# A graph-attention layer on one core: which operands of five vector steps lie in PSUM, and who issues the row loads and how the products are cut at the end

## The chip, the core and the metric

The kernel runs on one core of a Trainium2 chip. A core has five engines that run their own instruction streams: TensorE (PE, matrix products from SBUF into PSUM), VectorE (DVE), ScalarE (ACT), GpSimd (POOL) and SyncE (SP, which here only issues DMAs). SBUF and PSUM are the two on-chip memories of 128 partitions each. ACT and SP can also issue plain DMAs, one instruction each; POOL issues the indirect ones, which gather 128 rows of a table by 128 indices. Engines wait for each other through semaphores. The metric is device time in microseconds (us) of one launch; the median over several runs counts.

## The reference

One attention layer over a graph of 12,500 nodes and 412,500 edges that are sorted by their target, added to its input:

```python
h = jnp.maximum(_layernorm(x), 0.0)
h = (h @ W_node.T).reshape(N, 4, 32)
e = (edge_attr @ W_edge.T).reshape(E, 4, 32)
att = jnp.sum(jnp.concatenate([h[src], h[tgt], e], -1) * a, -1)
att = jnp.where(att > 0, att, 0.2 * att)
m = jnp.maximum(segment_max(att, tgt), 0.0)
ex = jnp.exp(att - m[tgt])
denom = segment_sum(ex, tgt) + (E - deg)[:, None] * jnp.exp(-m)
out = x + segment_sum((ex / denom[tgt])[:, :, None] * h[src], tgt)
```

The `0.2` is the leaky step that the change touches. The maximum per target is subtracted before the exponential, so sums of different pieces of one target have to be rescaled when they meet.

## The kernel before

**Data.** A preparation stage writes a table of one row per node (144 floats, 576 bytes): four heads of 32 projected features, two ones and a logit part (35 numbers per head, `AW`), and four more numbers per node. The edges are cut into 461 chunks of 7 tiles of 128 edges. Seven chunks are a batch (49 tiles); there are 66 batches, numbers 0 to 65, and the last has six chunks, the last of which has three tiles.

**Loading rows.** For each tile the 128 source rows come into a tile `hs`, of which there are three in a ring, so batch b+1 is loaded while b is worked on and the slot of b+1 was that of b-2. Most tiles are gathered by POOL (line 636 in `gather`, one indirect DMA each); ahead of a batch's gathers POOL does a tiny memset `gate` (line 631), which waits for the products of batch b-2. From batch 3 on the first tile of each odd batch and the first two of each even batch (the last batch: one) are instead loaded row by row with plain DMAs of 576 bytes (line 662 in `row_by_row`; line 658 loads 32 addresses into registers). Of each batch's 128 or 256 such rows, ACT issues 80 (`ACTROWS`) at the end of the iteration two before, SP the others: up to 64 at the start of the iteration before, then what is left, and with what remains of 112 those of the batch after next.

**One iteration b of the main loop**, in the order in which the code is written, which is also the order on each engine: SP's first rows of batch b+1, then its loads of `lw` for b+1 (line 585), POOL's gathers of b+1, SP's edge features for b+2, SP's other rows; then `weigh(b)`, which waits on DVE for the rows (line 670) and makes the weights; `load_pen` (SP, line 677), which has one buffer `pen_sb` and so waits for `weigh(b)`; `mark` (one-hot matrices, line 714); `scatter(b)` (DVE scales the rows, line 822, PE sums them per target, line 829); `spread` and `choose` for b+1 (lines 594 to 611); `begin(b+2)` (PE, edge logits into PSUM `z`, line 695). The sums of b-1 are copied by ACT within `weigh(b)` (`collect`, line 851) and merged into `acc` by `merge` every second batch; in the last four iterations that have it (from b = 62) `collect` and `close` of batch b itself stand at the end of iteration b, ahead of ACT's row issues for b+2. `finish` turns completed nodes into output.

**weigh_part** works on 32 partitions by 896 edges: four additions `att = z + zst` (line 751), the leaky step into `z` (754), a forward and a backward segmented maximum `up` and `m` (757, 759), a subtraction (760), four exponentials on ACT (762), four break products `both[.., 1]` from `pen` and `m` (766), transposes (768, 770). `z` and `up` are in PSUM, the others in SBUF.

**merge** makes decay factors `f` in the PSUM tile named "up", `scale` in SBUF, multiplies the sums `r` by `scale` (879), scans (881), writes products `put` in SBUF (888, 891) and adds them to two columns of `acc` per chunk (900).

**The last batch** (65) is weighed and multiplied in two parts, tiles 0 to 3 and 4 to 6, in `end_in_parts`: DVE scales the rows (796), PE makes one product of 32 by 140 per chunk and tile (802), and ACT copies it head by head, 32 by 35 each (810).

Of the kernel before, what the change touches and what calls it, by code (L numbers as in the profile page):

```python
# [14 lines left out]
OP = mybir.AluOpType  # L15
# [75 lines left out]
def by_row(b):  # L91

    return (2 if b % EVERY == 0 and b < NBT - 1 else 1) if LOOSE < b < NBT else 0


def merges():
# [36 lines left out]
def kernel(  # L133
# [603 lines left out]
    def weigh_part(s, t0, t1, before):  # L737

        zst, att, up, m, both = s.zst, s.att, s.up, s.m, s.both
        own = s.hs[:, :, :EROW].rearrange("p (t q) (h k) -> p t q h k", t=T, h=H)[:, t0:t1, :s.chunks, :, AW - 1]  # L740
        e0, e1 = t0 * P, t1 * P

        def grouped(what, g):
            return what.rearrange("r (t g i) -> r g t i", g=NQT, i=R)[:, g, t0:t1, :]

        nc.vector.tensor_tensor(logits[:, t0:t1, :s.chunks * H].rearrange("p t (q h) -> p t q h", h=H),  # L746
                                own, pick[:, t0:t1, :s.chunks, :H], op=OP.add)
        nc.vector.transpose(zst[:, t0:t1, :].rearrange("p t i -> p (t i)"),  # L748
                            logits[:, t0:t1, :].rearrange("p t i -> p (t i)"))
        for g in range(NQT):  # L750
            on_half(s, nc.vector.tensor_tensor(grouped(att, g), grouped(s.z, g),  # L751
                                               zst[g * R:(g + 1) * R, t0:t1, :], op=OP.add))
        z = s.z[:, e0:e1]
        on_half(s, nc.vector.scalar_tensor_tensor(z, att[:, e0:e1], 0.2, att[:, e0:e1], op0=OP.mult, op1=OP.max))  # L754
# [5 lines left out]
        on_half(s, nc.vector.tensor_tensor(att[:, e0:e1], z, mp, op=OP.subtract))  # L760
        for g in range(NQT):
            nc.scalar.activation(both[g * R:(g + 1) * R, 0, t0:t1, :], grouped(att, g), AF.Exp)  # L762
        if before:
            collect(before, 1)
        for g in range(NQT):
            nc.vector.scalar_tensor_tensor(both[g * R:(g + 1) * R, 1, t0:t1, :], grouped(s.pen[:, 1:], g), -1.0 / BIG,  # L766
                                           grouped(m, g), op0=OP.mult, op1=OP.mult)
        nc.vector.transpose(ex_ps[:, t0:t1, :].rearrange("p t r -> p (t r)"),  # L768
                            both[:, 0, t0:t1, :].rearrange("p t r -> p (t r)"))
        nc.vector.transpose(zst[:, t0:t1, :].rearrange("p t r -> p (t r)"),  # L770
                            both[:, 1, t0:t1, :].rearrange("p t r -> p (t r)"))
        nc.vector.tensor_copy(own, zst[:, t0:t1, :s.chunks * H].rearrange("p t (q h) -> p t q h", h=H))

    def end_in_parts(s):

        nc.vector.memset(s.pen[:, EARLY * P:EARLY * P + 1], -BIG)
        spans = ((0, EARLY), (EARLY, T))
        r = work.tile([P, AW * (MC + 1)], F32, name="r")
        r = r[:, :AW * (len(spans) * s.chunks + 1)].rearrange("p (d c) -> p d c", d=AW)
        breaks = work.tile([P, s.chunks, len(spans)], F32, name="breaks")  # L780
        nc.vector.memset(breaks, 0.0)
        nc.vector.tensor_copy(breaks[:, :, 0], new[:, s.c0:s.c0 + s.chunks])
        by_chunk = s.hs[:, :, :EROW].rearrange("p (t q) k -> p q t k", q=CB)
        for i, (t0, t1) in enumerate(spans):
            if i:
                landed(nc.vector, "late", late_sems, late_done, 0, s.hs[:, EARLY * CB:, :], s.ends[:, :, :, :])
                weigh_part(s, t0, t1, None)
            else:
                weigh(s, None)
            got = []  # L790
            for q in range(s.chunks):
                held = min(tiles_of(s.c0 + q), t1)
                if held <= t0:
                    continue
                rows = by_chunk[:, q, t0:held, :].rearrange("p t (h k) -> p t h k", h=H)[:, :, :, :HB]
                nc.vector.tensor_tensor(
                    rows, rows, ex_ps[:, t0:held, q * H:(q + 1) * H, None].to_broadcast([P, held - t0, H, HB]), op=OP.mult)
                if q % G == 0:
                    pa = ps.tile([P, RUN], F32, name="pa", bufs=3)
                at = q % G * W  # L800
                for t in range(t0, held):
                    nc.tensor.matmul(pa[at:at + W, :EROW], s.hot[:, t, q, :], s.hs[:, t * CB + q, :EROW],
                                     start=(t == t0), stop=(t == held - 1), tile_position=(0, at))
                got.append((q, pa[at:at + W, :]))
            for q in range(s.chunks):
                if tiles_of(s.c0 + q) <= t0:
                    nc.vector.memset(r[:, :, 1 + q * len(spans) + i], 0.0)
            for q, pa in got:
                for h in range(H):
                    nc.scalar.copy(r[h * W:(h + 1) * W, :, 1 + q * len(spans) + i], pa[:, h * AW:(h + 1) * AW])  # L810
        return r, breaks

    def scatter(s):
# [39 lines left out]
    def merge(c0, count, r, breaks=None):  # L853
# [2 lines left out]
        step = n // count  # L856
        breaks = new[:, c0:c0 + n] if breaks is None else breaks.rearrange("p c k -> p (c k)")
        flat = (AW - 1) * (n + 1)
        f = ps.tile([P, BANKS * 512], F32, name="up")[:, :flat].rearrange("p (d c) -> p d c", d=AW - 1)
        nc.vector.memset(f[:, :, 0], 0.0)  # L860
        m = r[:, AW - 1, 1:n + 1]
        run = work.tile([P, MC + 1], F32, name="run")
# [8 lines left out]
        nc.vector.tensor_tensor(dif[:, 0, :n], dif[:, 0, :n], breaks, op=OP.add)  # L871
        nc.vector.tensor_tensor(dif[:, 1, :n], m, run[:, 1:n + 1], op=OP.subtract)
        nc.scalar.activation(f[:, :HD + 1, 1:n + 1], dif[:, 0, None, :n].to_broadcast([P, HD + 1, n]), AF.Exp)
        scale = work.tile([P, MC], F32, name="scale")
        nc.scalar.activation(scale[:, :n], dif[:, 1, :n], AF.Exp)
        nc.vector.tensor_scalar(f[:, HD + 1, 1:n + 1], breaks, 1.0 / BIG, 1.0, op0=OP.mult, op1=OP.add)
        nc.vector.tensor_copy(r[:, :AW - 1, 0], carry)
# [196 lines left out]
    with tc.manual_schedule():  # L1074
# [15 lines left out]
        for b in range(NBT - 1):  # L1090
# [332 lines left out]
```

## Time and profile before

| what | value |
|---|---|
| median of 3 runs | 4031.48 us (4031.11 to 4036.24) |
| the profiled execution's own time | 4038.12 us |
| its span, first to last instruction | 4036.3 us |
| mean granted clock of TensorE | 0.679 |
| busy: POOL / DVE / PE / ACT | 75% / 59% / 36% / 22% of the span |

The profile is of one execution. A row of a group of instructions gives source line, engine, operation, output and inputs, count, then busy us and mean ns of one, then the idle time of the engine just before them and what ended it. A row of the timeline gives start and duration in us, engine, line, operation, output and inputs, count, and in brackets the idle time before it. SPq and ACTq are DMA issues on those engines' queues. The span's start is time zero in all of them.

### The profile page before, as it was taken

The numbers are of one execution on the slowest core, as the hardware profiler recorded it, in microseconds if no ns is written. First come the engines' busy times: TensorE is split into PE (matmuls) and PEld (weight loads), VectorE is DVE, ScalarE is ACT, GpSimd is POOL, SyncE is SP. The second block draws the span as 40 slices with busy tenths as digits, with TensorE's granted clock in tenths as the row PEclk, the third lists the DMA queues.
The fourth block names the chain that finished last, engine by engine and source line by source line (L and its number), as shares of the span: only waits on it lengthen the run. The fifth ranks groups of instructions, "written<-read, shape, count | busy, mean of one in ns | idle before, by whom it ended". The sixth has DMA issues, their size and how long they took to land.

```text
span 4036.3 us, 45376 instructions
## 1 busy us (share of the span) xinstructions
PE 1471.9 (36%) x3512; PEld 577.0 (14%) x3512; DVE 2379.0 (59%) x4319; ACT 875.2 (22%) x2714; POOL 3011.5 (75%) x3205
## 2 busy tenths in 40 slices
PE   5653334443243243333233234234323324324322
PEld 4311111111011011111011111111101101101101
DVE  8676666656555556546546646555655555655565
ACT  5232221222122212212212212212212211211222
POOL 7777777777777777777777777777777777777771
PEclk8776667776676676677576667666667667667666
DMA  8444444434434443334443343443443444343430
GB/s 223 121 102 114 117 109 110 101 93 103 109 90 109 108 110 91 101 88 107 108 110 93 100 103 91 108 109 95 99 107 90 105 108 109 87 105 89 109 92 23
DMA packets 287741, 418.29 MB, mean 104 GB/s; under 512 B 83154, under 2 KB 204430, under 8 KB 287410
## 3 DMA queue, kind: packets, MB, share of 16 engines
q0 software_dynamic: 100128, 230.32, 25.1%
q1 hardware_dynamic: 163696, 174.62, 14.8%
q10 hardware_dynamic: 23586, 10.39, 1.1%
q14 instruction: 301, 2.47, 0.2%
q8 instruction: 30, 0.49, 0.1%
HBM read 399.53 MB, written 15.51 MB: 103 GB/s over the span
## 4 chain that ended last, share of the span: by engine, by line
POOL 50%; issue 19%; DVE 6%; SPq 6%; ACTq 5%; PE 4%; ACT 2%; DMA 1%; DVEq 0%; POOLq 0%
POOL hs L636 50%; ACTq L662 4%; SPq L662 4%; PE pa L829 3%; DVE hs L822 2%; PE z L695 1%; SPq L658 1%; ACTq L658 1%; DMA hs<-table,ends 1%; ACT r L851 1%; ACT both L762 1%; DVE pick L611 1%; DVE hot L714 1%; DVE acc L900 1%; ACT up L986 1%
## 5 line engine op out<-in xcount | busy, mean ns | idle before, releaser
L636 POOL DMA_INDIRECT hs<-table,ends x3062 | 2938.8, 960 | 928.3 <-issue 924.7
L829 PE MATMUL pa<-hs,hot 128*128 128x502 f32 x1820 | 926.2, 673 | 2411.8 <-DVE hs L822 2333.8
L829 PEld LDWEIGHTS pa<-hs,hot 128*128 128x128 f32 x1820 | 396.3, 222 | 2933.8 <-issue 2863.7
L851 ACT COPY r<-pa 32x35 f32<-32x35 f32 x1820 | 380.0, 209 | 1968.7 <-issue 1882.8
L746 DVE TENSOR_TENSOR logits<-hs,pick 128x196 f32<-128x196 f32 (+1 forms) x67 | 32.9, 491 | 1017.2 <-DVEq L670 1016.6
L822 DVE TENSOR_TENSOR hs<-hs,exr 128x924 f32<-128x924 f32 x455 | 472.3, 1107 | 0.0
L695 PE MATMUL z<-eft,wa 128*32 128x512 f32 (+3 forms) x1056 | 443.6, 556 | 28.3 <-DMA eft<-in_ef 28.3
L611 DVE COPY_PREDICATED pick<-exr,lw 128x3136 f32<-128x3136 int32 x66 | 239.8, 3633 | 47.4 <-ACT pick L594 47.3
L611 DVE COPY_PREDICATED pick<-exr,pick 128x1568 f32<-128x1568 int32 (+3 forms) x198 | 230.6, 1165 | 6.8
L762 ACT ACTIVATE both<-a 32x224 f32<-32x224 f32 (+2 forms) x268 | 103.2, 385 | 599.2 <-DVE a L760 529.1
L594 ACT COPY pick<-lw 128x3136 f32<-128x3136 f32 x66 | 184.8, 2800 | 81.8 <-ACTq L670 80.3
L768 DVE STREAM_TRANSPOSE exr<-both 128x224 f32<-128x224 f32 (+1 forms) x67 | 28.3, 423 | 236.0 <-ACT both L762 236.0
L695 PEld LDWEIGHTS z<-eft,wa 128*32 128x32 f32 (+1 forms) x1056 | 95.6, 110 | 378.6 <-issue 353.7
L900 DVE TENSOR_TENSOR acc<-acc,a 128x70 f32 x461 | 108.0, 234 | 69.2 <-issue 50.9
L757 DVE TENSOR_TENSOR_SCAN up<-pen_sb,z 32x896 f32<-32x896 f32 (+1 forms) x67 | 133.3, 1990 | 11.9 <-DMA pen_sb<-pens 9.6
L714 DVE TENSOR_TENSOR hot<-exr,key 128x448 f32<-128x448 f32 (+1 forms) x260 | 129.0, 558 | 9.3 <-PE pa L829 2.3
L759 DVE TENSOR_TENSOR_SCAN m<-pen_sb,up 32x896 f32<-32x896 f32 (+1 forms) x67 | 132.6, 1979 | 2.3
L751 DVE TENSOR_TENSOR a<-z,zst 32x224 f32<-32x224 f32 (+2 forms) x268 | 101.0, 377 | 9.9 <-DVE zst L748 0.5
L766 DVE SCALAR_TENSOR_TENSOR both<-pen_sb,m 32x224 f32<-32x224 f32 (+2 forms) x268 | 100.8, 376 | 2.7
L986 ACT COPY up<-a 32x224 f32<-32x224 f32 (+1 forms) x224 | 74.5, 332 | 35.4 <-DVE a L978 28.7
L246 POOL DMA_INDIRECT hs<-in_x,ends x67 | 63.5, 948 | 20.5 <-issue 20.1
L754 DVE SCALAR_TENSOR_TENSOR z<-a 32x896 f32<-32x896 f32 (+1 forms) x67 | 72.1, 1075 | 2.3
(187 smaller groups left out, 1057.0 us busy)
## 6 DMA issues: line engine op xcount, KB each, us to landing
hs<-table SPq DMA_DIRECT2D x6992, 0.6 KB
eft<-in_ef SPq DMA_DIRECT2D x66, 1344.0 KB
hs<-table ACTq DMA_DIRECT2D x5040, 0.6 KB
hs<-table,ends POOLq DMA_INDIRECT x3062, 2.6
lw<-near SPq DMA_DIRECT2D x461, 64.0 KB
eft<-in_ef SPq DMA_DIRECT2D x66, 224.0 KB
pen_sb<-pens SPq DMA_DIRECT2D x66, 98.1 KB
table<-rows ACTq DMA_DIRECT2D x9, 648.0 KB
```

Of the source, the lines that this page charges most:

```text
L594: nc.scalar.copy(pick[:, :, :s.chunks, :], lw[:, None, :s.chunks, :n].to_broadcast([P, T, s.chunks, n]))
L611: nc.vector.copy_predicated(pick[:, :, :s.chunks, :n], bit[:, :, :, None].to_broadcast([P, T, s.chunks, n]), more)
L636: load = nc.gpsimd.indirect_dma_start(out=s.hs[:n, t * CB + q, :], out_offset=None, in_=table[:, :], in_offset=bass.IndirectOffsetOnAxis(a ...
L662: by_itself(engine.dma_start(s.hs[i % P:i % P + 1, i // P, :].bitcast(U8), table_b[ds(v, WIDE)].rearrange("(o c) -> o c", o=1)), f"lone{s. ...
L695: s.made = own_half(s, nc.tensor.matmul(s.z[:, part], wa3[:n, j, :], s.eft[:n, j, part], start=(j == 0), stop=(j == SB - 1)))
L714: nc.vector.tensor_tensor(s.hot[:, :, q0:q0 + n, :].rearrange("p t q r -> p q t r"), rows_ps[:, None, None, :].to_broadcast([P, n, T, W]), ...
L757: on_half(s, nc.vector.tensor_tensor_scan(up[:, e0:e1], s.pen[:, e0:e1], z, 0.0, op0=OP.add, op1=OP.max))
L762: nc.scalar.activation(both[g * R:(g + 1) * R, 0, t0:t1, :], grouped(att, g), AF.Exp)
L822: nc.vector.tensor_tensor(rows, rows, ex_ps[:, :, q * H:(q + 1) * H, None].to_broadcast([P, T, H, HB]), op=OP.mult)
L829: scattered[s.b] = nc.tensor.matmul(pa, s.hot[:, t, q0:q0 + G, :].rearrange("p q r -> p (q r)"), flat[:, at:at + RUN], start=(t == 0), sto ...
L851: nc.scalar.copy(to, pa[row:row + W, k:k + AW])
L900: nc.vector.tensor_tensor(cols, cols, put[:, i0 + i, :, :], op=OP.add)
```

## The change

Four vector steps get one of their two SBUF inputs into PSUM, the leaky step is cut in two for it, and two things change in the last batches:

- `weigh_part`: the sum of logits goes to the PSUM tile `up`; the leaky step becomes a multiplication `att = 0.2 * up` and a maximum of `up` and `att`; the break products read `up` (the forward maximum) where they read `m`, which is the same number wherever `pen` isn't zero.
- `merge`: `scale` and `put` lie in the PSUM tile "up".
- rows: `act_rows` gives ACT 40 rows of batch 64 and none of batch 65, instead of 80 of each; SP issues the others. SP's counts become 64 + 40 + 8 in iteration 63 (64 + 48 before) and 64 + 56 in iteration 64 (none before); its 112 in iteration 62 stay.
- `end_in_parts`: each product of 32 by 140 becomes four of 32 by 35, one per head, written to the head's own 32 partitions, with all chunks of a part side by side in one PSUM tile; ACT copies a part with one instruction, that of the first part after the second part's exponentials.

```diff
+def act_rows(b):
+    return ACTROWS if b < NBT - 2 else ACTROWS // 2 if b < NBT - 1 else 0
...
         for g in range(NQT):
-            on_half(s, nc.vector.tensor_tensor(grouped(att, g), grouped(s.z, g),
+            on_half(s, nc.vector.tensor_tensor(grouped(up, g), grouped(s.z, g),
                                                zst[g * R:(g + 1) * R, t0:t1, :], op=OP.add))
         z = s.z[:, e0:e1]
-        on_half(s, nc.vector.scalar_tensor_tensor(z, att[:, e0:e1], 0.2, att[:, e0:e1], op0=OP.mult, op1=OP.max))
+        nc.vector.tensor_scalar(att[:, e0:e1], up[:, e0:e1], 0.2, None, op0=OP.mult)
+        on_half(s, nc.vector.tensor_tensor(z, up[:, e0:e1], att[:, e0:e1], op=OP.max))
...
             nc.vector.scalar_tensor_tensor(both[g * R:(g + 1) * R, 1, t0:t1, :], grouped(s.pen[:, 1:], g), -1.0 / BIG,
-                                           grouped(m, g), op0=OP.mult, op1=OP.mult)
+                                           grouped(up, g), op0=OP.mult, op1=OP.mult)
...
+        sums = []
+        def keep(i):
+            nc.scalar.copy(r[:, :, 1 + i::len(spans)], sums[i])
         for i, (t0, t1) in enumerate(spans):
...
+            if i:
+                keep(i - 1)
+            pa = ps.tile([P, RUN], F32, name="pa", bufs=3)
+            sums.append(pa[:, :s.chunks * AW].rearrange("p (q d) -> p d q", d=AW))
             for q in range(s.chunks):
                 held = min(tiles_of(s.c0 + q), t1)
                 if held <= t0:
+                    nc.vector.memset(sums[i][:, :, q], 0.0)
                     continue
...
-                if q % G == 0:
-                    pa = ps.tile([P, RUN], F32, name="pa", bufs=3)
-                at = q % G * W
                 for t in range(t0, held):
-                    nc.tensor.matmul(pa[at:at + W, :EROW], s.hot[:, t, q, :], s.hs[:, t * CB + q, :EROW],
-                                     start=(t == t0), stop=(t == held - 1), tile_position=(0, at))
-                got.append((q, pa[at:at + W, :]))
...
-            for q, pa in got:
-                for h in range(H):
-                    nc.scalar.copy(r[h * W:(h + 1) * W, :, 1 + q * len(spans) + i], pa[:, h * AW:(h + 1) * AW])
+                    for h in range(H):
+                        nc.tensor.matmul(pa[h * W:(h + 1) * W, q * AW:(q + 1) * AW], s.hot[:, t, q, :],
+                                         s.hs[:, t * CB + q, h * AW:(h + 1) * AW],
+                                         start=(t == t0), stop=(t == held - 1), tile_position=(0, h * W))
+        keep(len(spans) - 1)
         return r, breaks
...
-        f = ps.tile([P, BANKS * 512], F32, name="up")[:, :flat].rearrange("p (d c) -> p d c", d=AW - 1)
+        up = ps.tile([P, BANKS * 512], F32, name="up")
+        f = up[:, :flat].rearrange("p (d c) -> p d c", d=AW - 1)
...
-        scale = work.tile([P, MC], F32, name="scale")
+        scale = up[:, 512:512 + MC]
...
-        put = work.tile([P, BUF], F32, name="a")[:, :MC * 2 * AW].rearrange("p (c j d) -> p c j d", c=MC, j=2)
+        put = up[:, :MC * 2 * AW].rearrange("p (c j d) -> p c j d", c=MC, j=2)
...
-                    row_by_row(batch(b + 2), nc.sync, ENG.SP, min(more, max(0, batch(b + 2).left - ACTROWS)))
+                    row_by_row(batch(b + 2), nc.sync, ENG.SP, min(more, max(0, batch(b + 2).left - act_rows(b + 2))))
...
-                row_by_row(batch(b + 2), nc.scalar, ENG.Activation, ACTROWS)
+                row_by_row(batch(b + 2), nc.scalar, ENG.Activation, act_rows(b + 2))
```

More of the change, by code (lines that the diff above doesn't have):

```diff
@@ L789, in end_in_parts @@
                 weigh(s, None)
-            got = []
+            if i:
+                keep(i - 1)
+            pa = ps.tile([P, RUN], F32, name="pa", bufs=3)
+            sums.append(pa[:, :s.chunks * AW].rearrange("p (q d) -> p d q", d=AW))
             for q in range(s.chunks):
@@ L797, in end_in_parts @@
                     rows, rows, ex_ps[:, t0:held, q * H:(q + 1) * H, None].to_broadcast([P, held - t0, H, HB]), op=OP.mult)
-                if q % G == 0:
-                    pa = ps.tile([P, RUN], F32, name="pa", bufs=3)
-                at = q % G * W
                 for t in range(t0, held):
-                    nc.tensor.matmul(pa[at:at + W, :EROW], s.hot[:, t, q, :], s.hs[:, t * CB + q, :EROW],
-                                     start=(t == t0), stop=(t == held - 1), tile_position=(0, at))
-                got.append((q, pa[at:at + W, :]))
-            for q in range(s.chunks):
-                if tiles_of(s.c0 + q) <= t0:
-                    nc.vector.memset(r[:, :, 1 + q * len(spans) + i], 0.0)
-            for q, pa in got:
-                for h in range(H):
-                    nc.scalar.copy(r[h * W:(h + 1) * W, :, 1 + q * len(spans) + i], pa[:, h * AW:(h + 1) * AW])
+                    for h in range(H):
[3 more added lines that the diff above has]
+        keep(len(spans) - 1)
         return r, breaks
```

## The prediction

> **What bounds the kernel now.** First the page: engine shares, then the costliest groups, then POOL's gather line by itself.
>
> ```profile
> PE 1471.9 (36%) x3512; PEld 577.0 (14%) x3512; DVE 2379.0 (59%) x4319; ACT 875.2 (22%) x2714; POOL 3011.5 (75%) x3205
> L636 POOL DMA_INDIRECT hs<-table,ends x3062 | 2938.8, 960 | 928.3 <-issue 924.7
> L636 POOL DMA_INDIRECT hs<-table,ends x3062: 939/947/1747, 86.9 to 3959.9; - x192
> ```
>
> POOL looks 75% busy, but its idle time ahead of the 3062 gathers is 0.30 us each and almost all "issue": nothing holds it. From 86.9 to 3960.9 us it issues one gather every 0.947 + 0.304 = 1.251 us. 3062 x 1.251 = 3831 of those 3874 us; the other 43 are longer gathers (longest 1747 ns). So two things set the time: POOL's stream, and what follows its last batches. The timeline shows what makes a gather long; here the first and the last of 54 alike, and a DVE step that does no harm:
>
> ```profile
> 155.03 1.09 DVE L754 SCALAR_TENSOR_TENSOR z<-a 32x896 f32<-32x896 f32 x1
> 155.22 1.72 POOL L636 DMA_INDIRECT hs<-table,ends  x1 [0.30 <-issue]
> 3925.07 1.09 DVE L754 SCALAR_TENSOR_TENSOR z<-a 32x896 f32<-32x896 f32 x1
> 3925.36 1.61 POOL L636 DMA_INDIRECT hs<-table,ends  x1 [0.30 <-issue]
> ...
> 3930.28 1.08 DVE L760 TENSOR_TENSOR a<-z,m 32x896 f32<-32x896 f32 x1
> 3931.03 0.94 POOL L636 DMA_INDIRECT hs<-table,ends  x1 [0.30 <-issue]
> ```
>
> The long gathers end 0.81 us after the leaky step's end (3926.16 to 3926.97). A normal one lasts 0.947, so a gather needs something 0.135 us after its start, and if DVE has it, POOL waits for the end of that instruction. Line 754 reads `a` twice, both SBUF. Line 760 reads one input from PSUM, was as long, ran across the same point (3931.17), and cost nothing. I matched all 185 gathers over 0.96 us (42.5 us of excess in all) to the DVE instruction that ended 0.81 us before their end. Line 754: 54 gathers, 28.9 us; 766: 57, 3.2; 879: 11, 2.7; 900: 20, 0.9. Those 35.7 us belong to the four steps changed. The other 6.8: 746 has 18 and 2.4, the last predicated copy of 611 (from `odd`) 14 and 2.0, 601 has 0.4, preparation the rest. Line 822 (`hs` with PSUM weights), in spite of 455 instructions, has no long one.
>
> ```profile
> L822 DVE TENSOR_TENSOR hs<-hs,exr 128x924 f32<-128x924 f32 x455 | 472.3, 1107 | 0.0
> L766 DVE SCALAR_TENSOR_TENSOR both<-pen_sb,m 32x224 f32<-32x224 f32 (+2 forms) x268 | 100.8, 376 | 2.7
> L754 DVE SCALAR_TENSOR_TENSOR z<-a 32x896 f32<-32x896 f32 (+1 forms) x67 | 72.1, 1075 | 2.3
> L746 DVE TENSOR_TENSOR logits<-hs,pick 128x196 f32<-128x196 f32 (+1 forms) x67 | 32.9, 491 | 1017.2 <-DVEq L670 1016.6
> L611 DVE COPY_PREDICATED pick<-odd,pick 128x196 f32<-128x196 int32 x66 | 25.1, 380 | 2.3
> L601 DVE TENSOR_TENSOR exr<-away,power 128x196 int32<-128x196 int32 x66 | 24.6, 373 | 5.1 <-ACT exr L561 2.8
> ```
>
> Then the end, ACT's timeline with DVE and POOL beside it:
>
> ```profile
> 3852.88 0.95 POOL L636 DMA_INDIRECT hs<-table,ends  x1 [0.30 <-issue]
> 3857.76 0.50 DVE L746 TENSOR_TENSOR logits<-hs,pick 128x196 f32<-128x196 f32 x1 [5.34 <-DVEq L670]
> 3847.93 32.92 ACTq L662 DMA_DIRECT2D hs<-table  x80
> 3880.89 1.59 ACT L762 ACTIVATE both<-a 32x224 f32<-32x224 f32 x4 [33.77 <-issue]
> 3912.87 0.95 POOL L636 DMA_INDIRECT hs<-table,ends  x1 [0.30 <-issue]
> 3922.64 0.37 DVE L746 TENSOR_TENSOR logits<-hs,pick 128x196 f32<-128x196 f32 x1
> 3923.41 31.24 ACTq L662 DMA_DIRECT2D hs<-table  x80
> 3954.70 1.59 ACT L762 ACTIVATE both<-a 32x224 f32<-32x224 f32 x4 [33.43 <-issue]
> ```
>
> Exponentials are ready when line 760 ends (3931.36, 8.7 us after 3922.64, plus 0.1), so batch 63's some 8.8 us after 3857.76; but ACT is issuing 80 rows until 3880.85. Batch 64's wait likewise, behind the rows of 65, until 3954.70. From there to the span's end (4036.3) lie 81.6 us of chained work.
>
> **POOL's stream, part by part.** Removing the four classes takes 35.7 us of stalls away. Three things come off. (a) The early gate:
>
> ```profile
> 235.38 14.36 PE L829 MATMUL pa<-hs,hot 128*128 128x502 f32 x28 [21.46 <-issue]
> 251.04 0.94 POOL L636 DMA_INDIRECT hs<-table,ends  x1 [0.76 <-DVE z L754]
> ```
>
> The gathers of batch 4 wait until batch 1's products end at 249.74. Those come after two `weigh`s in a row, each of which gains an instruction. The multiplication and the maximum should each cost what line 760 does, 1.08 plus 0.03 us between; both replace one, so +1.1 per batch, and this start slips by 2.2. The 1.4 us of stalls removed earlier become waiting there. (b) 0.7 us of the removed stalls lie in the last batch's gathers (3925.36 above), after 3914. (c) Stalls left over can grow: today's long gathers re-align POOL with DVE at each leaky step, and without that the 0.4 to 0.5 us instructions that still read two SBUF inputs meet the 0.135 us point by chance. Length squared over twice 1.251 is the mean stall: 0.096 us x 67 for 746, 0.058 x 66 for 611, 0.056 x 66 for 601, together 14.0 against 4.8 found, so 0 to 9.2 more. As 746 stands ahead of the leaky step and keeps its phase, I take 2.5. By gathers of 64: 35.7 - 1.4 - 2.2 - 0.7 - 2.5 = **29 us** earlier (22 to 31). DVE's added 1.1 us elsewhere is hidden by the 1016.6 us for which line 746 waits for rows; without that cover it would be 66 x 1.1 = 73. `up` is written and read by DVE in its own order, and ACT writes there only after DVE steps that it waits for already, so no wait is added.
>
> **The end.** Gathers of 64 end at 3913.8 - 29 = 3884.8. Their rows are waited for until 746 starts; for batch 63 that took 3857.76 - 3853.83 = 3.9 us, in other batches 2.5 to 6.8. With 4.0: 3888.8. The exponentials follow after 8.8 + 1.1: **3898.7** instead of 3954.70. This needs DVE and ACT free by then. Batch 63: 746 at 3857.76 - 28 = 3829.8, exponentials ready at 3839.7; ACT's 40 rows (16.5 us, half of 32.92) begin 26 us earlier than 3847.93 and end at 3838.4. From those exponentials to batch 64's 746 DVE and ACT work without a break for 3922.64 - 3880.89 = 41.8 us: 3881.5, 7 us before the rows. So the gathers decide. The rows moved onto SP cost
>
> ```profile
> 3826.42 23.13 SPq L662 DMA_DIRECT2D hs<-table  x64
> 3858.06 16.84 SPq L662 DMA_DIRECT2D hs<-table  x48
> 3897.84 2.73 SPq L585 DMA_DIRECT2D lw<-near  x6
> ```
>
> 0.36 us each: nothing new in iteration 63 (112 both times), and 120 x 0.36 = 43 us in iteration 64, behind which the loads of `lw` and `pen_sb` for 65 now queue on SP. SP is through with the rows of iteration 63 (3874.9 now) near 3850; with 43 more and the 23 that lie today between those rows and the next `lw` loads, rows and `pen_sb` are out by about 3918, and the last batch's first step is due 32.1 after 3898.7, at 3931. Hidden, with 13 us to spare. Its late gathers end 37 x 1.251 = 46.4 after 64's, at 3931, land by 3938, and are needed at 3943.
>
> In the last batch:
>
> ```profile
> 3995.94 6.03 PE L802 MATMUL pa<-hs,eft 128*32 128x140 f32 x46 [19.21 <-DVE hs L796]
> 4000.89 5.29 ACT L810 COPY r<-pa 32x35 f32<-32x35 f32 x24 [6.92 <-PE pa L802]
> 4002.78 0.55 DVE L760 TENSOR_TENSOR a<-z,m 32x384 f32<-32x384 f32 x1
> 4006.20 1.16 ACT L762 ACTIVATE both<-a 32x96 f32<-32x96 f32 x4
> 4009.11 3.16 PE L802 MATMUL pa<-hs,eft 128*32 128x140 f32 x30 [7.14 <-DVE hs L796]
> 4012.06 4.40 ACT L810 COPY r<-pa 32x35 f32<-32x35 f32 x20 [4.70 <-PE pa L802]
> 4016.49 0.17 DVE L865 TENSOR_SCALAR mc<-r 128x12 f32<-128x12 f32 x1 [5.51 <-ACT r L810]
> 4025.41 1.93 PE L988 MATMUL up<-a,ident 128*32 128x128 f32 x32 [13.14 <-DVE a L978]
> L802 PE MATMUL pa<-hs,eft x76: 282/441/442, 3995.9 to 4012.0; 128*32 128x140 f32 x76
> L802 PEld LDWEIGHTS pa<-hs,eft 128*32 128x32 f32 x76 | 6.8, 165 | 29.3 <-issue 27.4
> L398 ACT COPY rows<-ph 128x432 f32<-128x432 f32 (+1 forms) x33 | 16.8, 510 | 8.2 <-PE ph L391 7.3 <-ACT rstd L357 0.6
> ```
>
> 76 products become 304, 184 in part one and 120 in part two, each with its own weight load. No row has a product 35 wide. Nearest is line 988: 32 columns of weights, four positions in turn, 128 wide, 1.93/32 = 0.060 us each, loads included. Scaled to 35 columns that is 0.0165; the other end is a weight load that nothing overlaps, 0.165. I take 0.035, near the line 988 figures: 4.2 us for part two (0.131 each and 3.16 before). The 24 and 20 copies become one each of 128 x 210, 0.34 us between 220 (5.29/24) for 35 wide and 510 for 432, and the first no longer stands ahead of part two's exponentials. Those now follow line 760 (4003.33) at once, 2.9 us sooner; the extra leaky steps take back 0.7 + 0.6 (1.11 scaled by length, a fixed part kept). In the old clock: part two's products from 4007.6 to 4011.8, copy and latency 0.4, line 865 at 4012.2 instead of 4016.49: 4.3 us gained. At 0.060 it is 1.2, at 0.0165 5.6 (DVE's scaling then limits), at 0.165 a loss of 30.7.
>
> The Trainium skill speaks against cutting the products (TensorEngine Tiling (Array Packing), Instruction Overhead): a matmul one column wide takes as long as one of about 60, and a tiling factor should not come out of a dimension that is already small. By that estimate 35 columns cost what 60 do, 0.028 us instead of 0.0165 from line 988's row; the sum would move by under 1 us. No run here shows it yet.
>
> **Sum.** 3898.7 + 81.6 - 4.3 = 3976.0 for the span, 60.3 us less than 4036.3. The profiled execution took 4038.12 with 1.8 around its span, 6.6 more than the median shown; I carry the difference over: 4031.48 - 60.3 = **3971**. 29 of it is POOL's stream, 27 the rows off ACT (64's exponentials today come 40.9 us after its last gather's end, then 13.9), 4 the last batch's copies.
>
> **Rivals.**
> - SP becomes the bound. If its queue does not move up with POOL (it waits for `pen_sb` and buffers, not for gathers), rows and `pen_sb` of 65 are out near 3943 and the last batch starts 12 us late: 3983. For it: all moved rows lie past the loads of 65. Against: SP's waits end with DVE and PE steps that do move up.
> - PSUM doesn't relieve POOL, or the stall returns at the remaining two-input steps in full: minus 29 becomes 0, time 4000. Against: line 822's 455 instructions without one stall.
> - The rows don't free the end: something else holds batch 64's exponentials, and only 29 + 4 come: 3998. Against: both waits carry "issue" and 80 rows ahead of them.
> - Weight loads don't overlap (0.165 each): 3971 + 4.3 + 30.7 = 4006. Against: line 988's 0.060 with loads.
> - Slower than before: each of the four heads' products waits until the one ahead has left the array. Place: PE between lines 796 and 865. It decides from 0.248 us per product (304 x 0.248 = 75.5 us from 3996.6, which puts line 865 56 us late and eats all else). At the shortest isolated product, 0.282 us: 85.7 us, line 865 66 us late, 4042. For it: all four share one moving row block and successive ones are dependent on nothing but order; against: line 988's cadence, and 802's 0.131 where one product lasts 0.441.
>
> **Chances.** The forecast 0.72 (its own range 3963 to 3981: stall residue, landing 2.5 to 6.8, product cost up to 0.060); SP late 0.07; no relief 0.07; end not freed 0.06; loads serial 0.03; slower 0.03; the remaining 0.02 is a mixture that ends where it began. Range 3958 to 4001, which leaves out the last three and a little below. About 0.2% (8 us) is what a measurement of this kernel can tell from no change: faster 0.95, same 0.02, slower 0.03.
>
> **What would show it.** POOL's line 636: mean near 0.95 instead of 0.960, longest gather after 251 us under 1.5 us, none long at line 754's place; first gather of batch 4 near 253, last gather's end near 3931. ACT's exponentials for batch 64 near 3899 without rows ahead of them, SP's 120 rows done before 3925. In the last batch 304 products at 0.02 to 0.06 each, line 865 some 57 us after those exponentials. The prediction is wrong if long gathers stay at steps with one PSUM input, if line 746 of batch 64 or 65 waits for SP's rows, or if PE's 304 products take over 20 us.

## The result, and the profile after

| | before | after |
|---|---|---|
| median | 4031.3 us (4030.05 to 4036.24, 4 runs) | 3969.54 us (3967.33 to 3972.17, 4 runs) |
| profiled execution, own time / span | 4038.12 / 4036.3 us | 3967.33 / 3965.5 us |

The ratio of the times is 0.9843, with a 95% interval of 0.9827 to 0.9859: 62 us less, where 60 were forecast. The profiled executions stand 70.8 us apart in their spans, because the one of before lay 6.8 us above its median and the one of after 2.2 below.

From the page of the changed kernel: shares of the engines, then its groups by line (source line, engine, operation, tiles, count, busy us, mean ns, idle time before). Line 641 is the gather (636 before), 751 is the logits step (746), 759 and 760 are the two halves of the leaky step (754).

```profile
PE 1472.0 (37%) x3740; PEld 579.1 (15%) x3740; DVE 2455.5 (62%) x4386; ACT 867.8 (22%) x2672; POOL 2969.3 (75%) x3205
L641 POOL DMA_INDIRECT hs<-table,ends x3062 | 2896.7, 946 | 928.1 <-issue 923.4 <-DVE up L756 1.3 <-PE z L700 0.9
L751 DVE TENSOR_TENSOR logits<-hs,pick 128x196 f32<-128x196 f32 (+1 forms) x67 | 32.9, 491 | 842.4 <-DVEq L675 806.9 <-DMA eft<-in_ef 34.7
L760 DVE TENSOR_TENSOR z<-up,a 32x896 f32<-32x896 f32 (+1 forms) x67 | 72.0, 1075 | 2.3
L759 DVE TENSOR_SCALAR a<-up 32x896 f32<-32x896 f32 (+1 forms) x67 | 71.3, 1064 | 2.3
```

A gather's mean fell from 960 to 946 ns, and the median of all is 944, so hardly a long one is left. DVE is busy 76.5 us more, of which line 759 is 71.3. In exchange it waits less for rows: 842.4 us instead of 1017.2 ahead of the logits step, so its added work is hidden. POOL's share is the same 75% as before; only the length of its stream moved. The timeline shows the leaky step of batch 61, with the gathers beside it (start, duration in us):

```profile
3703.10 1.08 DVE L759 TENSOR_SCALAR a<-up 32x896 f32<-32x896 f32 x1
3703.25 0.94 POOL L641 DMA_INDIRECT hs<-table,ends  x1 [0.30 <-issue]
3704.22 1.09 DVE L760 TENSOR_TENSOR z<-up,a 32x896 f32<-32x896 f32 x1
3704.50 0.95 POOL L641 DMA_INDIRECT hs<-table,ends  x1 [0.30 <-issue]
```

Both instructions run across the point 0.135 us after a gather's start (3703.39, 3704.64), where line 754 held the gather until its own end; here the gathers last 0.94 and 0.95. Matched as in the prediction, the stalls sum to 7.1 us instead of 42.5: `odd` 19 with 2.2, logits 11 with 1.2, `power` 11 with 1.0, the rest preparation and crumbs. None stands at a changed step (leaky step, break products, the two steps of `merge`), and no gather after 251 us is longer than 1.222 us.

The end, from the timelines of DVE, ACT, SP and PE:

```profile
3820.15 15.79 ACTq L667 DMA_DIRECT2D hs<-table  x40
3835.99 1.59 ACT L768 ACTIVATE both<-a 32x224 f32<-32x224 f32 x4 [17.03 <-DVE a L766]
3851.16 23.37 SPq L667 DMA_DIRECT2D hs<-table  x64
3873.48 0.94 POOL L641 DMA_INDIRECT hs<-table,ends  x1 [0.31 <-issue]
3878.35 0.81 DVE L629 MEMSET hs<- 128x144 f32 x5
3879.08 0.37 DVE L751 TENSOR_TENSOR logits<-hs,pick 128x196 f32<-128x196 f32 x1
3881.35 20.28 SPq L667 DMA_DIRECT2D hs<-table  x56
3889.05 1.59 ACT L768 ACTIVATE both<-a 32x224 f32<-32x224 f32 x4 [11.33 <-DVE a L766]
3901.73 0.84 SPq L682 DMA_DIRECT2D pen_sb<-pens  x1
3919.70 0.94 POOL L641 DMA_INDIRECT hs<-table,ends  x1 [0.30 <-issue]
...
3941.93 2.28 PE L816 MATMUL pa<-hs,eft 128*32 128x35 f32 x120 [5.93 <-DVE hs L812]
3944.45 0.36 ACT L794 COPY r<-pa 128x210 f32<-128x210 f32 x1 [3.74 <-DVE pa L809]
3944.84 0.17 DVE L875 TENSOR_SCALAR mc<-r 128x12 f32<-128x12 f32 x1 [0.32 <-ACT r L794]
```

The exponentials of batch 64 stand at 3889.05, released by `a` and not by rows ("issue" before). The last gather of batch 64 ended at 3874.4, and the logits step of batch 64 follows DVE's own memsets without a wait. SP had the 120 rows and `pen_sb` out by 3902.6, 18 us before the last gather ended. From the exponentials to the span's end it takes 76.5 us (81.6 before).

### The profile page after: what moved, and what is told of

It is laid out like the page before. It is cut to its first block, busy times and chain, and to the rows that moved or that the text cites. A ratio compares the mean times of both kernels' runs of the same rounds, so it can differ in the third digit from the quotient of the medians.

```text
span 3965.5 us, 45886 instructions
## 1 busy us (share of the span) xinstructions
PE 1472.0 (37%) x3740; PEld 579.1 (15%) x3740; DVE 2455.5 (62%) x4386; ACT 867.8 (22%) x2672; POOL 2969.3 (75%) x3205
## 4 chain that ended last, share of the span: by engine, by line
POOL 44%; issue 18%; DVE 12%; ACTq 6%; SPq 5%; PE 4%; ACT 3%; DMA 2%; DVEq 1%; POOLq 0%
POOL hs L641 44%; ACTq L667 5%; SPq L667 3%; DVE hs L831 3%; PE pa L838 3%; DMA hs<-table,ends 1%; DVE pick L616 1%; ACTq L663 1%; PE z L700 1%; DVE acc L910 1%; ACT up L996 1%; SPq L663 1%; ACT r L860 1%; DVE hot L719 1%; ACT both L768 1%
## 5 line engine op out<-in xcount | busy, mean ns | idle before, releaser
L641 POOL DMA_INDIRECT hs<-table,ends x3062 | 2896.7, 946 | 928.1 <-issue 923.4
L751 DVE TENSOR_TENSOR logits<-hs,pick 128x196 f32<-128x196 f32 (+1 forms) x67 | 32.9, 491 | 842.4 <-DVEq L675 806.9
L910 DVE TENSOR_TENSOR acc<-acc,up 128x70 f32 x461 | 105.1, 228 | 90.2 <-issue 55.8
L756 DVE TENSOR_TENSOR up<-z,zst 32x224 f32<-32x224 f32 (+2 forms) x268 | 103.2, 385 | 14.1 <-DVE zst L753 0.5
L772 DVE SCALAR_TENSOR_TENSOR both<-pen_sb,up 32x224 f32<-32x224 f32 (+2 forms) x268 | 100.0, 373 | 3.8
L760 DVE TENSOR_TENSOR z<-up,a 32x896 f32<-32x896 f32 (+1 forms) x67 | 72.0, 1075 | 2.3
```

The costliest lines, as they stand in the source:

```text
L641: load = nc.gpsimd.indirect_dma_start(out=s.hs[:n, t * CB + q, :], out_offset=None, in_=table[:, :], in_offset=bass.IndirectOffsetOnAxis(a ...
L910: nc.vector.tensor_tensor(cols, cols, put[:, i0 + i, :, :], op=OP.add)
```

## The experiments

**The unchanged kernel again**, on the chip of the next three, for what differs between two executions. (The kernel before took 4033.99 us there, median of 11 runs.)

> The kernel before, unchanged. In the two profiles at hand the gathers that are not stalled take 945.8 ns (before) and 943.6 ns (changed) on average, which makes about 6.9 us over 2930 gathers. Theory: that is a difference between executions, not the change; this profile then shows 943.5 to 944.5 ns, a span near 4029, and the same 42 us of stalls, 54 or so of them at the leaky step of line 754. Rival: the change made every gather 2 ns shorter; then this profile shows 945.8 again and a span near 4036.

One execution: 4037.44 us, span 4035.5. Its gather, by line:

```profile
L636 POOL DMA_INDIRECT hs<-table,ends x3062: 940/944/1740, 87.0 to 3958.1; - x192
```

The median gather took 944 ns where the first execution of the same kernel had 947, while the stalls sum to 48.2 us instead of 42.5 (line 754 59 with 35.9, 766 61 with 3.5, 746 25 with 3.9). Both numbers differ between executions of one program. The shorter gathers did not shorten the span, which was expected near 4029: 6.7 us less gathering and 5.7 us more stalls nearly cancel. So neither of the two, at 6 or 7 us between two profiles, can be put down to an edit.

**Only the operands moved to PSUM** (leaky step, break products, `scale`, `put`); ACT keeps 80 rows, the last products stay 140 wide. This is the changed kernel with the other parts taken back; the edits of this section are shown in part, `...` stands for the rest.

```diff
 def act_rows(b):
-    return ACTROWS if b < NBT - 2 else ACTROWS // 2 if b < NBT - 1 else 0
+    return ACTROWS
...
```

> Only the four DVE steps with a PSUM input; rows and last products as before. Theory (two separate gains): POOL's last gather ends 33 us earlier than in the kernel before under the same conditions, stalls fall from 42 to 7 us, and the end follows by 25 to 31 us, less than POOL gains since ACT's 80 rows still stand ahead of batch 63's and 64's exponentials (33 us idle before each). Rival (one gain): nearly all of the 62 us comes from POOL and the rows were hidden anyway; then this run alone is 50 to 62 us faster.

Measured 4011.96 us (4011.15 to 4013.72), ratio 0.9947 (0.9932 to 0.9962): 22 us, a little under the 25 to 31 expected. ACT at the end, by its timeline:

```profile
3895.22 30.20 ACTq L667 DMA_DIRECT2D hs<-table  x80
3925.47 1.59 ACT L768 ACTIVATE both<-a 32x224 f32<-32x224 f32 x4 [32.36 <-issue]
```

Stalls fell to 6.6 us, and the last gather ended at 3922.1, 37 us before that of the unchanged kernel beside it. Less reaches the end: batch 64's exponentials come 29 us earlier (3954.47 there), the profiled execution ends 26 us earlier, the medians differ by 22. The logits step of the last batch came 36.9 us after its last gather: POOL had finished long ago, and ACT's rows held the exponentials.

**Only the rows moved from ACT to SP.**

```diff
-                row_by_row(batch(b + 2), nc.scalar, ENG.Activation, ACTROWS)
+                row_by_row(batch(b + 2), nc.scalar, ENG.Activation, act_rows(b + 2))
...
```

> Only act_rows: ACT issues 40 rows of batch 64 and none of 65. Theory: POOL's stream is as in the kernel before (last gather ends near 3954 to 3961), batch 64's exponentials start 5 to 15 us after the last gather of 64 ends instead of 41, and the time falls by 24 to 30 us. Rival (rows hidden): within 5 us of the kernel before, the end set by the last gathers. Rival (SP is late): SP's 120 rows end after 3925 and the gain is under 15 us.

Measured 4000.94 us (3999.88 to 4002.69), ratio 0.9919 (0.9904 to 0.9935): 33 us, more than the 24 to 30 expected. ACT and DVE at the end:

```profile
3844.34 15.93 ACTq L667 DMA_DIRECT2D hs<-table  x40
3860.32 1.59 ACT L767 ACTIVATE both<-a 32x224 f32<-32x224 f32 x4 [16.79 <-DVE both L771]
3908.14 0.50 DVE L751 TENSOR_TENSOR logits<-hs,pick 128x196 f32<-128x196 f32 x1 [6.71 <-DVEq L675]
3917.04 1.59 ACT L767 ACTIVATE both<-a 32x224 f32<-32x224 f32 x4 [17.04 <-DVE a L765]
```

The exponentials of batch 64 follow `a` and come 37.4 us before those of the unchanged kernel (3954.47). In the profiled execution the last gather also ended 7 us earlier (3951.9 instead of 3959.1; stalls of 41 us instead of 48), which this edit doesn't explain. Now the gathers are last: the logits step of batch 64 waits 6.71 us for rows of which the last gather ended at 3904.33. The place at which the chain of waits leaves POOL shows how the two parts stand to each other; first the kernel before, then this one:

```profile
3791.26 3.21 DMA hs<-table,ends
3903.39 4.11 DMA hs<-table,ends
```

The first line is the last gather of batch 62, the second that of batch 64. In the kernel before, POOL sets the time up to batch 62, and from there DVE's and ACT's chain with ACT's rows in it does. The two stand one behind the other, so that one edit doesn't hide the other.

**Only the last batch's products cut by head** and copied by one instruction per part.

```diff
-                    nc.tensor.matmul(pa[at:at + W, :EROW], s.hot[:, t, q, :], s.hs[:, t * CB + q, :EROW],
-                                     start=(t == t0), stop=(t == held - 1), tile_position=(0, at))
+                    for h in range(H):
+                        nc.tensor.matmul(pa[h * W:(h + 1) * W, q * AW:(q + 1) * AW], s.hot[:, t, q, :],
+                                         s.hs[:, t * CB + q, h * AW:(h + 1) * AW],
+                                         start=(t == t0), stop=(t == held - 1), tile_position=(0, h * W))
...
```

> Only the last batch's products cut by head and copied at once. Theory: 304 products at 0.02 us each, two copies instead of 44, 5 to 7 us faster; from batch 64's exponentials to the end 75 to 76 us instead of 81.6. Rival: weight loads of 0.165 us each, 25 us or more slower.

Measured 4024.82 us (4020.49 to 4027.52), ratio 0.9977 (0.9965 to 0.9988): 9 us, with 5 to 14 in the interval (5 to 7 were expected).

```profile
3951.47 1.59 ACT L762 ACTIVATE both<-a 32x224 f32<-32x224 f32 x4 [33.45 <-issue]
4003.20 2.28 PE L810 MATMUL pa<-hs,eft 128*32 128x35 f32 x120 [5.95 <-DVE hs L806]
4005.72 0.36 ACT L788 COPY r<-pa 128x210 f32<-128x210 f32 x1 [3.89 <-DVE pa L803]
4006.11 0.17 DVE L868 TENSOR_SCALAR mc<-r 128x12 f32<-128x12 f32 x1 [0.33 <-ACT r L788]
```

From the exponentials of batch 64 to the first step of the last merge it is 54.6 us, where it was 61.8 in the first profile of the kernel before and 61.2 in the second: about 7 us by this edit. In the last part the copies shrank from 4.40 to 0.36 us and the products from 3.16 to 2.28; the two were not tried apart. A product costs 2.28/120 = 0.019 us with its weight load. The page on TensorEngine Tiling (Array Packing) of the Trainium skill (Instruction Overhead) would have 35 columns cost what 60 do, in the prediction's estimate 0.028 us; these products, which go to four positions in turn, issue faster than that, and the measurement decides. The sum of the three parts alone is 22 + 33 + 9 = 64 us, the whole gives 62: within their intervals they add up.

**Which operand holds a gather.** Four kernels were then run twice. Both times they fell on other chips, where the kernel before took 6977.63 us (median of 35 runs) and 7020.68 us (31 runs), so none of the times forecast for them could be tested; which steps hold gathers could be. First the kernel before with the leaky step alone in PSUM (the additions ahead of it write `up`):

```diff
...
-        on_half(s, nc.vector.scalar_tensor_tensor(z, att[:, e0:e1], 0.2, att[:, e0:e1], op0=OP.mult, op1=OP.max))
+        nc.vector.tensor_scalar(att[:, e0:e1], up[:, e0:e1], 0.2, None, op0=OP.mult)
+        on_half(s, nc.vector.tensor_tensor(z, up[:, e0:e1], att[:, e0:e1], op=OP.max))
```

> The kernel before with one part of the change: only the leaky step becomes a multiplication and a maximum that read PSUM; break products, merge steps, rows and the last batch's products stay as before. Theory (a gather waits for the end of a DVE instruction that reads two SBUF inputs and is running 0.135 us after the gather's start): no long gather at the two new steps, so the 36 us of the unchanged kernel at line 754 go; 6 to 18 us stay at the other steps (746, 766, 879, 900), last gather end near 3930 (3925 to 3938), 3 to 15 us later than with all four classes relieved (3922). The end follows ACT's 80 rows as it did there, so the time falls by 12 to 22 us. Rival (the sum over all four classes counts, none by itself): less than half of the 36 us goes, last gather end past 3940, less than 10 us gained.

> The kernel before with the leaky step alone in two instructions that read PSUM, where a row by SP or ACT costs the 0.36 to 0.41 us of the first runs. Theory (the two new steps hold no gather): the 36 us at line 754 go, 6 to 18 us are left at 746, 767 and 880, last gather end 3925 to 3938. ACT's 80 rows still hold the end, so 12 to 22 us faster than before. Rival (the sum over all four classes counts): last gather end past 3940, less than 10 us gained. If rows cost near 1 us here too: POOL waits some 50 us per batch and no difference over 0.5%.

Then the kernel before with the same split, all of it in SBUF:

```diff
-        on_half(s, nc.vector.scalar_tensor_tensor(z, att[:, e0:e1], 0.2, att[:, e0:e1], op0=OP.mult, op1=OP.max))
+        nc.vector.tensor_scalar(m[:, e0:e1], att[:, e0:e1], 0.2, None, op0=OP.mult)
+        on_half(s, nc.vector.tensor_tensor(z, att[:, e0:e1], m[:, e0:e1], op=OP.max))
```

> The kernel before with the leaky step split in the same two instructions, but with `a` and the scaled copy both in SBUF: the multiplication reads one SBUF input, the maximum two. Theory (two SBUF inputs hold a gather): long gathers stand at the maximum, about as many as at line 754 before (40 to 67 with 20 to 40 us in all), total of stalls 35 to 60 us, last gather end 3955 to 3975, time within 10 us of before on either side. If the multiplication, SBUF to SBUF, holds gathers as well, its own 10 to 30 us come on top and the time rises by 5 to 20 us. Rival (the split itself helps, whatever memory is read): stalls and time as in the kernel with the leaky step alone in PSUM, last gather end near 3930, 12 to 22 us faster.

> The kernel before with the leaky step split in two, all operands in SBUF. From the first run of it: the maximum (two SBUF inputs, 1.08 us) and the multiplication (SBUF to SBUF, 0.616 us) both hold gathers. With POOL without a pause, each batch's pair meets one or two gathers: 25 to 55 us of stalls at the pair, 35 to 65 in all, last gather end 3950 to 3975, and with ACT's 80 rows at the end a time within 10 us of before on either side. Rival (splitting relieves by itself): stalls under 20 us in all, last gather end near 3930, 12 to 22 us faster.

The other two are the changed kernel with line 754 of before put back (first fence), and the changed kernel with `odd` and `power` in PSUM as well (second):

```diff
...
-        nc.vector.tensor_scalar(att[:, e0:e1], up[:, e0:e1], 0.2, None, op0=OP.mult)
-        on_half(s, nc.vector.tensor_tensor(z, up[:, e0:e1], att[:, e0:e1], op=OP.max))
+        on_half(s, nc.vector.scalar_tensor_tensor(z, att[:, e0:e1], 0.2, att[:, e0:e1], op0=OP.mult, op1=OP.max))
```

```diff
...
+    power_ps = bank[:, BITS + (LEVELS - 1) * T * CB:].bitcast(I32)
+    nc.vector.tensor_copy(power_ps, power[:, :LEVELS - 1])
...
-    odd = work.tile([P, CB * T], I32, name="odd")
...
+        odd = ps.tile([P, BANKS * 512], F32, name="up")[:, :CB * T].bitcast(I32)
```

> The changed kernel with line 754 of before put back: one instruction that reads `a` twice from SBUF; all else as changed. Theory: 50 to 60 long gathers with 28 to 38 us return there and nowhere else, last gather end 3948 to 3958 instead of 3921. As rows no longer hold ACT at the end, nearly all of it reaches the end: 3990 to 4000, that is 33 to 44 us faster than before instead of 62. Rival (at the end ACT or the last batch's chain decides, not POOL): under 15 us of the gain lost, below 3985.

> The changed kernel with the one-instruction leaky step that reads `a` twice from SBUF put back. Theory: 28 to 38 us of stalls return there and nowhere else, last gather end 3948 to 3958 instead of 3921; as rows no longer hold ACT at the end, nearly all of it reaches the end: 3990 to 4000, 33 to 44 us faster than before instead of 62. Rival (at the end the DVE and ACT chain or the last batch decides, not POOL): under 15 us of the gain lost, below 3985.

> The changed kernel with two more two-input steps fed from PSUM: `odd`, which the last predicated copy reads, and the bit masks `power`. Theory: their stalls (2.2 and 1.0 us of the changed kernel's 7.1) go, 3 to 5 us of stalls are left (746's and preparation's), last gather end 2 to 4 us before 3921. Batch 64's first step stood behind DVE's own work and not behind its rows, so at most half of it reaches the end: time 0 to 3 us below the changed kernel's 3969.5, which cannot be told from no difference. Rival (POOL still decides the end): 3 us or more faster, with line 746 of batches 64 and 65 earlier by as much as the gathers.

> The changed kernel with `odd` and the bit masks `power` in PSUM as well. Theory: 2 to 4 us of stalls instead of 7.1, last gather end 3 to 5 us earlier than 3921, and as batch 64's first step stood behind DVE's own work, at most half of it at the end: 0 to 3 us below the changed kernel, 58 to 66 us faster than before. Rival (POOL still decides the end): 65 to 70 us faster, with line 754 of batches 64 and 65 earlier by as much as the gathers.

What was measured, first run and second run of each; the stalls are matched as before, and the leaky step's own are of 67 instructions each:

| kernel | ratio to before on its chip (95%) | all stalls, us | at the leaky step: long gathers and us |
|---|---|---|---|
| leaky step in PSUM | 1.0034 (1.0021 to 1.0047); 1.0035 (1.0016 to 1.0054) | 8.6; 6.8 | none; none |
| leaky step split in SBUF | 1.0004 (0.9992 to 1.0017); 0.9996 (0.9982 to 1.001) | 25.9; 27.9 | multiplication 23 with 5.2; 27 with 6.2. Maximum 24 with 11.6; 24 with 11.5 |
| changed, old leaky step | 0.9971 (0.9956 to 0.9985); 0.9971 (0.996 to 0.9983) | 20.7; 24.4 | 39 with 17.1; 37 with 18.6 |
| changed, more in PSUM | 1.0008 (0.9995 to 1.002); 0.9988 (0.9975 to 1.0001) | 2.7; 3.9 | none; none |

The stalls at the pair (17 and 18 us) and at the old leaky step (17 and 19) stay under the 25 to 55 and 28 to 38 expected, which were for a POOL that never pauses; here it does, as shown below. Where they stand is the same on these chips, and the first two rows tell the theories apart. The second run of the kernel split in SBUF, two stretches of its timeline and then its groups by line:

```profile
751.14 0.61 DVE L754 TENSOR_SCALAR m<-a 32x896 f32<-32x896 f32 x1
751.31 1.27 POOL L636 DMA_INDIRECT hs<-table,ends  x1 [0.30 <-issue]
...
2002.93 1.18 POOL L636 DMA_INDIRECT hs<-table,ends  x1 [0.30 <-issue]
2002.96 0.38 DVE L751 TENSOR_TENSOR a<-z,zst 32x224 f32<-32x224 f32 x1
2004.03 1.09 DVE L755 TENSOR_TENSOR z<-a,m 32x896 f32<-32x896 f32 x1
2004.42 1.51 POOL L636 DMA_INDIRECT hs<-table,ends  x1 [0.30 <-issue]
```

```profile
L755 DVE TENSOR_TENSOR z<-a,m 32x896 f32<-32x896 f32 (+1 forms) x67 | 72.1, 1077 | 3.0 <-issue 0.8
L754 DVE TENSOR_SCALAR m<-a 32x896 f32<-32x896 f32 (+1 forms) x67 | 41.0, 612 | 3.3 <-issue 1.0
```

The gather beside the multiplication ends about 0.82 us after the multiplication's end, and the one beside the maximum (2005.93) 0.81 after the maximum's (2005.12). So splitting alone relieves nothing. And the multiplication, which reads one SBUF input, holds gathers too; it runs in 0.612 us where the one from PSUM takes 1.064. The Trainium skill (SBUF — State Buffer, Who interferes with whom) states both: two SBUF inputs contend with a GpSimd instruction that reads SBUF, and so does a `tensor_scalar` in a mode that uses both read ports. These rows agree, but for one step. The prediction's rule, two SBUF inputs, was half of it.

That step is line 751 at 2002.96, the last of the four additions, which reads one input from PSUM and stands just ahead of the SBUF multiplication. In the two runs of this kernel 15 of 15 and 14 of 15 gathers that it met were long, and ended 0.77 us after it; in the kernel before, where line 754 follows the same addition, none of 19 was. What holds them is open. In the changed kernel, where the addition is followed by the multiplication from PSUM, none of 25 was long.

With the old leaky step put back, long gathers return there (39 and 37 of 67), with up to 1.74 us, while 766 and 879 stay clean: the classes are separate. `odd` and `power` in PSUM lose theirs as well; what is left then is mostly the logits step and the preparation. What this last kernel is worth beside the changed one where rows are cheap was not measured.

**What the other chips show.** The second run of the kernel with the leaky step alone in PSUM, four of its groups by line and then its timeline of SP and ACT:

```profile
L636 POOL DMA_INDIRECT hs<-table,ends x3062 | 2903.7, 948 | 1110.6 <-issue 930.0 <-DVE hs L624 81.3 <-DMA table<-rows 72.0
L746 DVE TENSOR_TENSOR logits<-hs,pick 128x196 f32<-128x196 f32 (+1 forms) x67 | 33.0, 492 | 9.2 <-issue 0.8 <-DVEq L670 0.7
L631 POOL MEMSET gate<- 128x1 f32 x63 | 6.3, 100 | 2823.8 <-PE pa L830 2799.3 <-remote 24.4
L769 DVE STREAM_TRANSPOSE exr<-both 128x224 f32<-128x224 f32 (+1 forms) x67 | 28.4, 423 | 2465.2 <-ACT both L763 2275.1 <-issue 190.1
```

```profile
3999.31 53.33 ACTq L662 DMA_DIRECT2D hs<-table  x22
3999.73 117.03 SPq L662 DMA_DIRECT2D hs<-table  x112
```

Gather, gap and DVE steps last what they did; a row by SP costs 117.03/112 = 1.04 us instead of 0.365 (23.37/64 above). POOL waits at its gate for 2824 us, and the logits step for 9 us instead of 1017: POOL is no longer the bound. Row loads on SP and ACT are 23% and 17% of the chain that ends last, and DVE now waits 2465 us for ACT's exponentials. DVE's waiting has thus moved from ahead of the logits step to behind the added instruction, where some of it can still hide that instruction. There the PSUM form of the leaky step makes the kernel slower by 0.34 and 0.35% (21 to 25 us), though it holds no gather at that step. The prediction put 73 us on the added work without cover; about a third of it came. That the added DVE time is the cause is argued from these rows only: the split in SBUF adds 41 us of DVE work and showed no loss beyond 0.17%. The whole change, with two more operands moved, made no difference there that can be told from none (1.0008 and 0.9988), and with the old leaky step it was 0.29% faster than the kernel before, both times.

## Why the prediction was right, step by step

- **What bounds the kernel: right.** POOL's stream, and behind its last batches the chain through ACT's rows, one after the other: the operands alone gave 22 us, the rows alone 33.
- **The stalls of four classes, 35.7 us: right.** None is left at any of the four, and the leaky step's come back with its old form. A detail of the matching was off: the long gathers at the logits step end 0.77 us after it and not 0.81.
- **What comes off: the gate right, the residue too large.** The first gather of batch 4 started at 252.21 (253.2 forecast):

```profile
237.34 13.56 PE L838 MATMUL pa<-hs,hot 128*128 128x502 f32 x28 [22.87 <-issue]
251.03 0.10 POOL L636 MEMSET gate<- 128x1 f32 x1 [2.25 <-PE pa L838]
252.21 0.94 POOL L641 DMA_INDIRECT hs<-table,ends  x1 [1.08 <-DVE up L756]
```

  Today's other stalls were to grow by 2.5; they went from 6.8 to 7.1.
- **Gathers of 64 end at 3884.8: 3874.4, 10.4 earlier.** 7 of these are the gather itself: 943.6 ns unstalled instead of 945.8, from start to start 1248.8 instead of 1251.2, over 3062. The unchanged kernel's second execution has the same 943.6, so this belongs to the execution, not to the change. The gate gave 1.0, the residue 2.2.
- **"So the gathers decide": the step that failed.** With gathers 10 us earlier than forecast, DVE's and ACT's chain from batch 62 on was last, by little: the logits step of batch 64 (3879.08) waited for nothing, 4.7 us after the gathers. That chain began late as well, at 3764.80, 9.3 us after the last gather of batch 62 ended and not 4. The chain of waits, in order of time, and then SP's timeline:

```profile
3754.51 9.92 DMA hs<-table,ends
```

```profile
3742.39 0.50 SPq L581 DMA_DIRECT2D eft<-in_ef  x1
3742.94 0.81 SPq L582 DMA_DIRECT2D eft<-in_ef  x1
```

  The last gather of that batch needed 9.92 us from its start until its rows had landed, with 1.3 MB of edge features issued 12 us ahead of it. That these held it up is a guess; it wasn't tried, and in the profile of before such a load stood 14.5 us ahead of the same gather, which needed 3.21. From the logits step to the exponentials it took 9.97 us (9.9 forecast).
- **Rows on SP hidden: right.** Rows and `pen_sb` were out at 3902.6 (3918 forecast). The 40 rows left on ACT were just few enough: they ended at 3835.94, where batch 63's exponentials (3835.99) could have started at 3835.7.
- **The last batch: right, its product mis-sized.** 0.019 us instead of 0.035. From batch 64's exponentials to the first step of the last merge: 61.8 before, 57.5 forecast, 55.8 measured; 54.6 without the two longer leaky steps, which thus cost 1.2 (1.3 forecast). 0.9 of that gain is lost behind it, so 81.6 became 76.5 (77.3 forecast).
- **The split into 29 + 27 + 4** is that of one order in which they are made. Alone they gave 22, 33 and 9.
- **The sum, 3971 against 3969.5**, is nearer than its steps: the span fell by 70.8 us and not by 60.3. Most of what was missed is the 7 us by which the two executions differ; carrying the profiled execution's distance to its median over, as was done, assumed that the second would lie as high. That the sum comes within 2 us is partly luck: the gathers of batch 64 and the chain were done within a few us of each other, so that naming the wrong one of them cost little.

None of the rivals came: SP's loads were early, the 304 products took 6 us in all, weight loads ran beside them.

## What to carry to other kernels

When one engine generates gathers without a pause, look for gathers that end a fixed time after a vector instruction, and move one operand of that instruction to PSUM; a multiplication from SBUF to SBUF held them as well, and splitting alone didn't help. Follow the chain of waits to the place at which it changes engines: a stream and the chain behind it stand one after the other, and here the gains on them added up (22, 33 and 9 us alone, 62 together). What is bought with another engine's slack may cost as soon as that slack is gone: price the added step without its cover before making the edit.

## What the hardware showed beyond expectation

- The unstalled gather's 943.6 or 945.8 ns, and the stalls' 42 to 48 us, vary between executions of one kernel.
- The same plain 576-byte loads cost their issuing engine, register loads included, about 0.36 us each on SP and 0.39 to 0.41 on ACT in the profiles of before and after, and 1.04 in the stretch shown of one of the other chips, while the transfers took no longer. Queue rows of the page, of the second run of the kernel with the leaky step in PSUM:

```profile
q1 hardware_dynamic: 163696, 174.62, 8.5%
```

  8.5% of 7031 us is 598 us per DMA engine; the unchanged kernel of the first experiment had 14.7% of 4035.5, 593 us, for as many packets. Most starts of successive rows still stand 0.32 us apart there, but for long stretches 2.80 us, on SP and ACT alike. What paces them is open.
- Products of 35 columns that go to four positions in turn issue every 0.019 us, weights included.
- An addition with one PSUM input held 29 of the 30 gathers that it met, where an SBUF multiplication stood behind it, and none of 19 without; why is open.
